# A four-layer kernel: layer 2's mixing reordered with its slot inputs one quarter ahead, its row sums moved a step earlier, and layer 3's value products paired

## The chip, the cores and the metric

The kernel runs on one core of a Trainium2 chip, as one program. The metric is the device time in microseconds (us). The profile is one execution of that program, recorded by the hardware profiler; "the span" is the time from its first to its last recorded instruction. The engines are named as the profile names them: PE (matmul) with PEld (its weight loads), DVE (vector), ACT (scalar), POOL (GpSimd) and SP (which here issues DMAs). Each engine executes its own queue in order; a semaphore makes one wait for another.

## What is computed

2,048 tokens of 512 channels go through four layers, each of the form x = x + ffn(cond(x)): attention with experts (layer 0), 32 experts with 4 chosen per token (layer 1), a soft mixture of experts (layer 2), and attention over a paged cache with an int8 product (layer 3). The change lies in the end of layer 1 and in layers 2 and 3; their lines are these, cut:

```python
# layer 1, the last step: every token sums its K = 4 expert rows
outs = outs[inv].reshape(-1, K, Hh)
y = jnp.sum(outs * topk_weight[..., None], axis=1)
# layer 2, cond: a base product and a low-rank adapter per sequence
H = jnp.einsum('btd,od->bto', x, W);  xa = jnp.einsum('btd,brd->btr', x, A_b)
delta = jnp.einsum('btr,bor->bto', xa, B_b) * s_b
# layer 2, ffn: 16 experts of 128 slots
logits = jnp.einsum('bnd,des->bnes', x_n, mu_n)
dispatch = jax.nn.softmax(logits, axis=1)                      # over a sequence's tokens
combine = jax.nn.softmax(logits.reshape(B, N, E * S), axis=-1) # over all slots
slot_in = jnp.einsum('bnd,bnes->besd', x_ln, dispatch)
h = gelu(jnp.einsum('besd,edh->besh', slot_in, W1) + b1)
slot_out = jnp.einsum('besh,ehd->besd', h, W2) + b2
out = jnp.einsum('bsd,bns->bnd', slot_out, combine)
# layer 3: scores over the gathered cache, softmax, values
o = jnp.einsum('bghts,bgsd->bghtd', softmax(scores), v_all)
```

In the kernel a tile holds two sequences of 64 tokens; layer 2 runs over 16 tiles and, within a tile, over its 16 experts in four quarters of four.

## The kernel before

**Tiles and layers.** The stream is 16 tiles of 128 tokens by 512 channels, kept in DRAM between layers. Layers 0 and 1 run first. Layer 1 leaves the experts' rows in DRAM (`ys`), and layer 2 sums them when it fetches a tile: tile load `xt` on SP, four gathers `yk` of 128 rows on POOL, and four adds on DVE, x += gate * yk (L1295 in `fetch` and `add`; L1280 in `combined`, which does the first two tiles at the head of layer 2 before anything else). The gathers' buffers `yk` are four, the tiles' buffers `xt` three.

**Layer 2** (`layer2`, L1752) is a loop of 17 steps. Step i works on two tiles at once: the first half of tile i (its softmaxes) and the second half of tile i - 1 (its mixing), while the base product and norm of tile i + 1 (`Lora`, `l2_norm_pieces`) run between. Most instructions are pinned, so that each engine's queue stands nearly as the source has it. The rest is placed by a scheduler. A step is, on PE:

- **logits**: four quarters of 16 matmuls `lp` (L1995), each scaled, maximised and exponentiated behind it (DVE L2000 to L2021, ACT L2024); two transposes `ep` (L2081) of the other tile's softmax come between.
- **hidden**: four quarters `zp` of 4 matmuls (L2072) for the other tile; DVE reads each into `z` (L2074). The bank `zp` has two buffers. Between them stand `tp2` (L2039), the highest logit of each row, from which DVE makes `dg` (L2043), and `bp` (L2049), the product with `dg` that spreads it. In this part, too, stand the four adds of the tile that is being fetched: two behind `z` 0, two behind `dg`.
- **mixing** of the other tile: `csum` and `dp` (the softmax's total), and for each quarter q: `turn(q)` (`ep`, copied to `ew` by ACT, L2083), `dispatch(q)` (`hp`, 8 matmuls, L2104, then two GELUs into `h` on ACT, L2109), `combine(q)` (`gp`, 16 matmuls, L2127, copied to `gT` by DVE, L2131) and `project(q)` (4 matmuls `out` of 128x512, L2138). `hp` and `gp` have one buffer each, `ew` and `gT` two, `h` three (each quarter uses two). Between them stand `Lora` and the pieces of the next norm: DVE L1957 to L1965, POOL L396 and L1967 (times gamma, plus beta), ACT L1972 (the square), POOL L396, DVE L1975 to L1978.

The order of the mixing is written out by hand (L1817 to L1889), in short: combine 0, dispatch 1, turn 3, project 0, combine 1, dispatch 2, project 1, combine 2, dispatch 3, project 2, combine 3, the transpose of the next tile, the bias product (L2143), project 3.

In its free stretches POOL also copies cache rows for layer 3 (`cache_rows`, `kvst`: a gather, then a store by SP; one buffer).

**Layer 3** (`Attend`, L2587) is a software pipeline of 64 steps, one for each sequence and pair of head groups. Step s does on PE: `kp`, the transposed keys of step s + 3; `pT`, the transposed probabilities of step s (`turn0`, `turn1`; six buffers `pTs`); `sp`, the scores of step s + 2; one output product `y` (L2700); and `op`, the value product of step s - 1 (L2678: three chunks for each of two heads, into one bank), which ACT copies to `oT` (L2681).

**Branches.** After layers 0 and 1 a conditional block (L1061) handles the pairs beyond the experts' capacity; here there are none, and all engines branch over it. Three tiles before the end of the expert stage `hint` (L315) marks the branch as likely taken on PE, DVE, ACT and POOL.

Of the kernel before, what the change touches and what calls it, by code (L numbers as in the profile page):

```python
# [10 lines left out]
F32 = mybir.dt.float32  # L11
# [5 lines left out]
ALU = mybir.AluOpType  # L17
# [4 lines left out]
P = 128  # L22
B, T, D = 32, 64, 512
NT = B * T // P
# [6 lines left out]
E1, K1, V1 = 32, 4, 56  # L31
# [218 lines left out]
class Prog:  # L250
# [43 lines left out]
    def results(self, pool):  # L294
# [16 lines left out]
                )  # L311

        return step

    def hint(self, label):  # L315

        traced = self.nc.cur_bb.bb.instructions
        before = len(traced)
        kinds = mybir.EngineType
        self.tc.mark_branch_hint_location(  # L320
            label, "LikelyTaken", (kinds.PE, kinds.DVE, kinds.Activation, kinds.Pool)
        )
        for ins in list(traced)[before:]:
            self.pin(SimpleNamespace(ins=ins))

    def pin(self, ins):

# [528 lines left out]
class Moe:  # L856
# [193 lines left out]
    def beyond(self):  # L1050
# [7 lines left out]
            number[0:1, 0:1], min_val=0, max_val=N * K,  # L1058
            skip_runtime_bounds_check_because="the number of pairs is at most N * K",
        )  # L1060
        with tc.If(n > 0, label=f"beyond{E}"), ExitStack() as ctx:  # L1061
            sb = ctx.enter_context(tc.tile_pool(name=f"vs{E}", bufs=1))
            ps = ctx.enter_context(tc.tile_pool(name=f"vps{E}", bufs=2, space=PSUM))
            iota = g.c("iota")
# [90 lines left out]
    def run(self, xs, per_tile):  # L1155
# [7 lines left out]
        with ExitStack() as ctx:  # L1163
# [77 lines left out]
            for u in range(len(self.units)):  # L1241
                k = 0
# [51 lines left out]
        def add(x, yk, gate):  # L1294
            g.pin(nc.vector.scalar_tensor_tensor(x, yk, gate, x, ALU.mult, ALU.add))  # L1295

        combined.fetch, combined.moe = fetch, self
        return combined
# [453 lines left out]
def layer2(g, w, combined, first, w3):  # L1752
    tc, nc, a = g.tc, g.nc, g.a
    with ExitStack() as ctx:
# [8 lines left out]
        x = [combined(sb, 0, 3), combined(sb, 1, 3)]  # L1763
# [20 lines left out]
        for i in range(NT + 1):  # L1784
            soft = Softmaxes(g, w, sb, s2, ps, xnT) if i < NT else None
            mix = Mix(g, w, sb, s2, ps, x[i - 1], *last) if last else None
            adds = []
            if len(x) < NT and i != 1:
                t, adds = combined.fetch(sb, max(i + 1, 2), 3)
                x.append(t)  # L1790
            if mix and not soft:
                mix.turn(0)
# [18 lines left out]
            if early:  # L1811
                lora.turn()
                mix.sums()
                lora.adapter()
                soft.highest()
                soft.divide(3)
                mix.dispatch(0)  # L1817
                norm = l2_norm_pieces(g, w, sb, s2, lora.product())
                next(norm)
                mix.total()  # L1820
                soft.over_slots()
                mix.turn(2)
                mix.combine(0)
                mix.dispatch(1)
            else:
                if z:
                    z.hidden(0)
                if soft:
                    soft.divide(3)
                for add in adds[0:2]:  # L1830
                    add()
# [5 lines left out]
                for add in adds[2:4]:  # L1837
                    add()
                if z:
                    z.hidden(2)  # L1840
                if soft:
                    soft.over_slots()
                if z:
                    z.hidden(3)
                    next(rows, None)
            if mix and not early:
                if lora:
                    lora.turn()
                mix.sums()
                mix.dispatch(0)  # L1850
                if lora:
                    lora.adapter()
                mix.turn(2)
                if lora:
                    norm = l2_norm_pieces(g, w, sb, s2, lora.product())
                    next(norm)
                    if i + 2 == NT:

                        w3["w_kv3"] = first.tile([P, 4, D], F32, name="w_kv3", tag="sb_w_2")
                        g.dma(w3["w_kv3"], a["w_kv3"])  # L1860
                        w3["x3"] = [first.tile([P, D], F32, name="x3", tag=f"sb_{k}") for k in ("w_a", "w_b")]
                        for j in range(2):
                            g.dma(w3["x3"][j], xs[j * P : (j + 1) * P, :])
                mix.total()
                mix.combine(0)
                mix.dispatch(1)
            if mix:
                mix.turn(3)
                if lora:
                    next(norm)  # L1870
                mix.project(0)
                next(rows, None)
                mix.combine(1)
                if lora:
# [7 lines left out]
                mix.combine(3)  # L1882
            before = xnT, nn
# [171 lines left out]
class Mix:  # L2055
# [76 lines left out]

    def project(self, q):
        g, nc, w = self.g, self.g.nc, self.w
        if q == 0:
            self.out = self.ps.tile([P, D], F32, name="out2", tag="acc", bufs=1)
        for e in range(4):
            g.first(e, nc.tensor.matmul(  # L2138
                self.out, self.gTs[q][:, e, :], w["w2"][:, 4 * q + e, :], start=q + e == 0, stop=q + e == 6 and q == 3
            ))  # L2140

    def bias(self):
        self.g.pin(self.g.nc.tensor.matmul(self.out, self.cs, self.w["b2"], start=False, stop=False))  # L2143

    def finish(self, xs, xb, i):
        g, nc, x = self.g, self.g.nc, self.x
# [208 lines left out]
def layer3(g, w, xs, xb):  # L2355
# [3 lines left out]
    with ExitStack() as ctx:  # L2359
# [159 lines left out]
        for s in range(-3, last + 8):  # L2519
# [67 lines left out]
class Attend:  # L2587
# [79 lines left out]
    def values(self, s):  # L2667

        nc = self.g.nc
        i, gp, half = self.where(s)  # L2670
        if s % 4 == 0:
            self.oT[i] = self.sb.tile([P, 2, 2, P], F32, name="oT", bufs=3)
        kv, pT = self.kvs[2 * i + half], self.pT.pop(s)
        op = self.ps.tile([P, P], F32, name="op", tag="op", bufs=1)
        for c in range(3):
            for j in range(2):
                at = 256 + (2 * gp + j) * 64
                nc.tensor.matmul(  # L2678
                    op[64 * j : 64 * j + 64, :], kv[c][:, at : at + 64], pT[j][:, c, :], start=c == 0, stop=c == 2
                )  # L2680
        nc.scalar.copy(  # L2681
            self.oT[i][:, gp, :, 64 * half : 64 * half + 64], op.rearrange("p (h t) -> p h t", h=2)
        )
        if half:
            self.products += [partial(self.product, i, 2 * gp + k) for k in range(2)]

    def out(self):

# [76 lines left out]
```

## Time and profile before

| what | us |
|---|---|
| median of 3 runs (lowest to highest) | 2591.81 (2587.51 to 2593.32) |
| the profiled execution: its time | 2598.3 |
| the profiled execution: its span | 2596.5 |
| head of layer 2, 1140.0 to 1228.0: PE busy | 67.6 of 88.0 |
| layer 2, the steps of tiles 1 to 14, 1292.6 to 2113.8: PE busy | 800.8 of 821.2 |
| layer 3, the attention steps, 2329.3 to 2596.5: PE busy | 253.9 of 267.2 |
| the same stretch: DVE busy, ACT busy | 209.9, 163.1 |

The page has six parts: busy time by engine, the span in 40 slices, DMA queues, the chain of work that ended last, the costliest groups of instructions, and DMA issues. A row of the timeline has the start in us, the time from the first to the last of the instructions merged in it, the engine, the line, the operation, out<-in, their number, and in brackets how long the engine was idle before it and what released it. Every matmul of this kernel appears as two passes, so 4 matmuls are x8 in a row. A PE row's length runs to the modelled end of its last pass, which lies a little behind the start of the next row; where PE time is counted here, it is from the start of one row to the start of the next.

### The profile page before, as it was taken

To read this page: it belongs to the slowest core of one execution; us is meant where nothing else is said; L and a number is where in the kernel's file an instruction comes from. 1 tells how busy PE (TensorE), PEld (TensorE's weight loads), DVE (VectorE), ACT (ScalarE), POOL (GpSimd) and SP (SyncE) were. 2 spreads that over 40 slices of the span, in tenths; PEclk is the share of its full clock that TensorE was granted. 3 is DMA by queue.
4 is the path that set the end of the run, shared out by engine and by line. 5 is a ranking of instruction groups with operands and counts; after the bars stand their busy time and mean duration, and the time that the engine had idled before them with its cause. 6 is when DMAs were issued, how large, how long until landed. Compare 5 with 4: busy or idle time off the path is not lost.

```text
span 2596.5 us, 42488 instructions
## 1 busy us (share of the span) xinstructions
PE 2447.1 (94%) x16582; PEld 1617.0 (62%) x16597; DVE 1411.3 (54%) x3470; ACT 718.1 (28%) x1512; POOL 904.0 (35%) x961
## 2 busy tenths in 40 slices
PE   6999979998799999979999999999999999979998
PEld 4777766666566666747666666666666665445554
DVE  4666646833745554447444444444444442657886
ACT  2444521112211111102222222222222221246664
POOL 2223225504144444523333333333333312563440
PEclk9999989998889999989999999999999999989999
DMA  2335225535456976844222222222222314424441
GB/s 102 108 120 186 92 98 181 190 103 194 162 198 227 362 273 238 283 128 148 72 72 72 72 75 68 79 72 72 75 73 74 96 56 138 167 58 132 134 136 46
DMA packets 132568, 339.39 MB, mean 131 GB/s; under 512 B 23993, under 2 KB 25049, under 8 KB 125056
## 3 DMA queue, kind: packets, MB, share of 16 engines
q1 hardware_dynamic: 90720, 188.84, 21.2%
q0 software_dynamic: 41056, 141.89, 17.2%
q10 hardware_dynamic: 576, 5.77, 0.6%
q8 instruction: 136, 2.23, 0.3%
q14 instruction: 80, 0.66, 0.1%
HBM read 245.23 MB, written 107.22 MB: 136 GB/s over the span
## 4 chain that ended last, share of the span: by engine, by line
PE 43%; DVE 10%; issue 2%; POOL 1%; DMA 0%; ACT 0%; another core or an unknown queue 0%; POOLq 0%; ACTq 0%; SPq 0%; DVEq 0%
PE out L2138 9%; PE lp L1995 7%; PE gp L2127 3%; PE pp L2452 3%; PE zp L2072 3%; PE yp L1938 2%; PE y L2700 2%; PE hp L2104 2%; PE op L2678 2%; PE sp L2631 2%; PE pT L2653 2%; DVE xt L1295 1%; PE ep L2081 1%; DVE inv L2031 1%; PE kp L2604 1%
## 5 line engine op out<-in xcount | busy, mean ns | idle before, releaser
L1202 PE MATMUL gu<-xT,wt 128*128 128x320 f32 (+5 forms) x1536 | 397.7, 406 | 4.6 <-DVE xT L1189 3.6
L1202 PEld LDWEIGHTS gu<-xT,wt 128*128 128x128 f32 x1536 | 283.6, 193 | 118.9 <-issue 49.1
L2138 PE MATMUL out<-sb_w,gT 128*128 128x512 f32 x512 | 233.6, 599 | 11.0 <-DVE nn L1975 6.5
L1995 PEld LDWEIGHTS lp<-xnT,sb_mu 128*128 128x128 f32 x2048 | 233.4, 192 | 9.3 <-issue 6.7
L1995 PE MATMUL lp<-xnT,sb_mu 128*128 128x128 f32 x2048 | 236.4, 275 | 2.1 <-DVE xnT L344 1.4
L2072 PE MATMUL zp<-sb_w,xnT 128*128 128x512 f32 x512 | 228.5, 595 | 3.6 <-DVE z L2074 3.6
L1217 PE MATMUL y<-wt,hT 128*128 128x512 f32 (+2 forms) x544 | 201.6, 599 | 2.7 <-DVE yo L1225 2.1
L372 POOL DMA_INDIRECT kvst<-kv,gidx x96 | 96.5, 1005 | 278.9 <-DMA oldkv<-kvst 194.0
L2131 DVE COPY gT<-gp 128x512 f32<-128x512 f32 x64 | 44.2, 691 | 246.0 <-PE gp L2127 245.6
L2138 PEld LDWEIGHTS out<-sb_w,gT 128*128 128x128 f32 x512 | 93.2, 190 | 116.1 <-issue 95.2
L2072 PEld LDWEIGHTS zp<-sb_w,xnT 128*128 128x128 f32 x512 | 93.7, 190 | 111.6 <-issue 99.5
L372 POOL DMA_INDIRECT kvt<-newkv,oidx x96 | 100.4, 1046 | 132.4 <-DMA kvt<-oldkv 77.8
L372 POOL DMA_INDIRECT yk<-ys,slot x96 | 97.5, 1015 | 116.3 <-DVE pre L1307 74.5
L2109 ACT ACTIVATE h<-hp 128x512 f32<-128x512 f32 x128 | 69.5, 595 | 213.6 <-PE hp L2104 213.5
L1217 PEld LDWEIGHTS y<-wt,hT 128*128 128x128 f32 (+2 forms) x544 | 73.3, 167 | 65.6 <-issue 52.4
L372 POOL DMA_INDIRECT xr<-rows,stok x101 | 98.2, 972 | 40.4 <-issue 18.3
L852 POOL TENSOR_TENSOR ga<-ga,sg 128x288 f32<-128x288 f32 (+5 forms) x66 | 50.8, 770 | 173.6 <-ACT sg L848 171.6
L2149 POOL TENSOR_TENSOR xt<-xt,bc_bias 128x512 f32<-128x512 f32 x16 | 20.2, 1264 | 220.5 <-DMA x<-xt 208.4
L2000 DVE TENSOR_TENSOR lT<-lp,cmu 128x512 f32<-128x512 f32 x64 | 43.5, 680 | 93.8 <-PE lp L1995 92.8
L2033 POOL TENSOR_TENSOR eT<-eT,inv 128x512 f32<-128x512 f32 x64 | 71.8, 1123 | 54.3 <-DVE inv L2032 46.2
L2127 PEld LDWEIGHTS gp<-lT,h 128*64 128x64 f32 x2048 | 65.0, 138 | 38.9 <-issue 25.9
L2024 ACT ACTIVATE eT<-eT 128x512 f32<-128x512 f32 x64 | 40.3, 630 | 173.9 <-DVE eT L2021 154.2
(458 smaller groups left out, 4642.9 us busy)
## 6 DMA issues: line engine op xcount, KB each, us to landing
ys<-yo SPq DMA_DIRECT2D x106, 256.0 KB
oldkv<-kvst SPq DMA_DIRECT2D x96, 224.0 KB
kvt<-oldkv SPq DMA_DIRECT2D x96, 224.0 KB
ys<-zero SPq DMA_DIRECT2D x10, 2048.0 KB
xt<-x SPq DMA_DIRECT2D x62, 256.0 KB
x<-xt SPq DMA_DIRECT2D x48, 256.0 KB
wt<-w_e SPq DMA_DIRECT2D x7, 1536.0 KB
sb_w<-w SPq DMA_DIRECT2D x5, 1024.0 KB
```

The costliest lines, as they stand in the source:

```text
L372: ins = self.nc.gpsimd.indirect_dma_start(out=out, out_offset=None, in_=src, in_offset=bass.IndirectOffsetOnAxis(ap=idx, axis=0), **kw)
L1202: follow(nc.tensor.matmul(o, wj[:, c, ic * P : (ic + 1) * P], xTs[u][:, c, 0:n], start=c == 0, stop=c == 3))
L1217: follow(nc.tensor.matmul(y[row : row + n, :], hTs[e][:, ic, col : col + n], wd[:, ic, :], start=ic == 0, stop=ic == 1,))
L1938: g.first(c, nc.tensor.matmul(yp, self.xT[:, c, :], w["w_2"][:, c, :], start=c == 0, stop=False))
L1995: g.first(e + c, nc.tensor.matmul(lp[:, e, :], w["mu"][:, c, (4 * q + e) * P : (4 * q + e + 1) * P], self.xnT[:, c, :], start=c == 0, stop ...
L2033: g.pin(nc.gpsimd.tensor_tensor(e3, e3, inv.unsqueeze(2).to_broadcast([P, 8, T]), ALU.mult))
L2072: g.first(c, nc.tensor.matmul(zp, self.xnT[:, c, :], w["w1"][:, c, cols], start=c == 0, stop=c == 3))
L2104: g.first(e + b, nc.tensor.matmul(hp[:, b, e, :], self.ews[q][r, e, :], self.z[q][r, e * P : (e + 1) * P], start=True, stop=True))
L2109: g.pin(nc.scalar.activation(self.hs[q][b], hp[:, b], AF.Gelu))
L2127: g.first(e + b + k, nc.tensor.matmul(gp[r, e, cols], self.hs[q][b][:, e, r], self.lT[q][:, e, cols], start=True, stop=True))
L2138: g.first(e, nc.tensor.matmul(self.out, self.gTs[q][:, e, :], w["w2"][:, 4 * q + e, :], start=q + e == 0, stop=q + e == 6 and q == 3))
L2452: nc.tensor.matmul(pp, xT[i][:, c, :], (w["w_kv3"] if z else wq)[:, c, :], start=c == 0, stop=c == 3)
```

## The change

- **Mixing.** The order becomes: dispatch 1, combine 0, the bias product, turn 3, dispatch 2, combine 1, project 0, dispatch 3, combine 2, project 1, combine 3, project 2, the transpose, project 3. The bias product now opens the accumulation (start=True) and project 0 no longer does. The early branch (step 1) and the other steps share it.
- **Row sums.** Step i fetches tile i + 2 (before: tile i + 1, and none at step 1). In steps from 1 on the adds stand in the mixing: behind the norm's first piece, behind combine 1, ahead of dispatch 3 and behind combine 3; at step 0 they stay in the hidden part. Three gathers go out at the fetch; the fourth is issued behind the first add. `yk` has three buffers instead of four (in `combined` too), `xt` four instead of three.
- **Layer 3.** `values` runs at even steps only, for two steps at once: 12 matmuls into one bank of twice the width, one ACT copy of 256 columns instead of two of 128.
- **Branches.** `hint` and the branch's label are gone.

As built, the orders of PE and DVE in a step are those of the source. On ACT, where the square of the norm (L1972) is not pinned, the order in the mixing changes from "GELUs of 1, `ew` 3, square, GELUs of 2" to "GELUs of 1, square, `ew` 3, GELUs of 2". On POOL the fourth gather stands behind the norm's last operation and ahead of two `kvst` gathers, and the other three open the step. On SP the load of tile 3 moves up next to that of tile 2, and every later one by one step.

```diff
-        with tc.If(n > 0, label=f"beyond{E}"), ExitStack() as ctx:
+        with tc.If(n > 0), ExitStack() as ctx:
...
-                if t == self.tiles - 3:
-                    g.hint(f"beyond{E}")
...
-                yk = pool.tile([P, D], F32, name="yk", bufs=4 if K == K1 else 6)
+                yk = pool.tile([P, D], F32, name="yk", bufs=3 if K == K1 else 6)
...
             adds = []
-            for k in range(K):
-                yk = pool.tile([P, D], F32, name="yk", bufs=4)
+
+            def rows(k):
+                yk = pool.tile([P, D], F32, name="yk", bufs=3)
                 g.gather(yk, self.ys, self.slot[:, i, k : k + 1], later=True)
-                adds.append(partial(add, x, yk, self.gates[:, i, k : k + 1]))
+                adds.append(partial(add, yk, k))
+
+            def add(yk, k):
+                g.pin(nc.vector.scalar_tensor_tensor(x, yk, self.gates[:, i, k : k + 1], x, ALU.mult, ALU.add))
+                if len(adds) < K:
+                    rows(len(adds))
+
+            for k in range(3):
+                rows(k)
             return x, adds
...
-            if len(x) < NT and i != 1:
-                t, adds = combined.fetch(sb, max(i + 1, 2), 3)
+            if len(x) < NT:
+                t, adds = combined.fetch(sb, i + 2, 4)
...
-                mix.combine(0)
-                mix.dispatch(1)
...
                 mix.total()
+            if mix:
+                mix.dispatch(1)
                 mix.combine(0)
-                mix.dispatch(1)
-            if mix:
-                mix.turn(3)
                 if lora:
                     next(norm)
-                mix.project(0)
+                add(0)
+                mix.bias()
+                mix.turn(3)
+                mix.dispatch(2)
                 next(rows, None)
                 mix.combine(1)
+                add(1)
+                mix.project(0)
+                add(2)
+                mix.dispatch(3)
+                mix.combine(2)
                 if lora:
                     xn = next(norm)
-                mix.dispatch(2)
                 mix.project(1)
-                mix.combine(2)
-                mix.dispatch(3)
-                mix.project(2)
                 next(rows, None)
                 mix.combine(3)
+                add(3)
+                mix.project(2)
...
             if mix:
-                mix.bias()
                 mix.project(3)
...
-            if 0 <= s - 1 <= last:
-                f.values(s - 1)
+            if s % 2 == 0 and 0 <= s - 2 <= last:
+                f.values(s - 2)
```

More of the change, by code (lines that the diff above doesn't have):

```diff
@@ L313, in results @@
         return step
[L315 to L324, printed above, removed]
     def pin(self, ins):
@@ L1287, in fetch @@
             adds = []
-            for k in range(K):
-                yk = pool.tile([P, D], F32, name="yk", bufs=4)
+            def rows(k):
+                yk = pool.tile([P, D], F32, name="yk", bufs=3)
                 g.gather(yk, self.ys, self.slot[:, i, k : k + 1], later=True)
-                adds.append(partial(add, x, yk, self.gates[:, i, k : k + 1]))
+                adds.append(partial(add, yk, k))
[5 more added lines that the diff above has]
+                rows(k)
             return x, adds
-        def add(x, yk, gate):
-            g.pin(nc.vector.scalar_tensor_tensor(x, yk, gate, x, ALU.mult, ALU.add))
         combined.fetch, combined.moe = fetch, self
@@ L1762, in layer2 @@
         xs, xb = g.stream("x2"), g.stream("x2b")
-        x = [combined(sb, 0, 3), combined(sb, 1, 3)]
+        x = [combined(sb, 0, 4), combined(sb, 1, 4)]
         for k in ("gamma", "beta"):
@@ L1787, in layer2, with add @@
             adds = []
-            if len(x) < NT and i != 1:
-                t, adds = combined.fetch(sb, max(i + 1, 2), 3)
+            def add(k):
+                if k < len(adds):
+                    adds[k]()
+            if len(x) < NT:
+                t, adds = combined.fetch(sb, i + 2, 4)
                 x.append(t)
@@ L1829, in layer2 @@
                     soft.divide(3)
-                for add in adds[0:2]:
-                    add()
+                if i == 0:
+                    add(0)
+                    add(1)
                 if z:
@@ L1836, in layer2 @@
                     soft.highest()
-                for add in adds[2:4]:
-                    add()
+                if i == 0:
+                    add(2)
+                    add(3)
                 if z:
@@ L1864, in layer2 @@
                 mix.total()
+            if mix:
+                mix.dispatch(1)
                 mix.combine(0)
-                mix.dispatch(1)
-            if mix:
-                mix.turn(3)
                 if lora:
                     next(norm)
-                mix.project(0)
+                add(0)
+                mix.bias()
+                mix.turn(3)
+                mix.dispatch(2)
                 next(rows, None)
                 mix.combine(1)
+                add(1)
+                mix.project(0)
+                add(2)
+                mix.dispatch(3)
+                mix.combine(2)
                 if lora:
                     xn = next(norm)
-                mix.dispatch(2)
                 mix.project(1)
-                mix.combine(2)
-                mix.dispatch(3)
-                mix.project(2)
                 next(rows, None)
                 mix.combine(3)
+                add(3)
+                mix.project(2)
             before = xnT, nn
@@ L2134, in project @@
         g, nc, w = self.g, self.g.nc, self.w
-        if q == 0:
-            self.out = self.ps.tile([P, D], F32, name="out2", tag="acc", bufs=1)
         for e in range(4):
             g.first(e, nc.tensor.matmul(
-                self.out, self.gTs[q][:, e, :], w["w2"][:, 4 * q + e, :], start=q + e == 0, stop=q + e == 6 and q == 3
+                self.out, self.gTs[q][:, e, :], w["w2"][:, 4 * q + e, :], start=False, stop=q + e == 6 and q == 3
             ))
     def bias(self):
-        self.g.pin(self.g.nc.tensor.matmul(self.out, self.cs, self.w["b2"], start=False, stop=False))
+        self.out = self.ps.tile([P, D], F32, name="out2", tag="acc", bufs=1)
+        self.g.pin(self.g.nc.tensor.matmul(self.out, self.cs, self.w["b2"], start=True, stop=False))
     def finish(self, xs, xb, i):
@@ L2669, in values @@
         nc = self.g.nc
-        i, gp, half = self.where(s)
-        if s % 4 == 0:
+        i, gp, _ = self.where(s)
+        if gp == 0:
             self.oT[i] = self.sb.tile([P, 2, 2, P], F32, name="oT", bufs=3)
[L2673 to L2680, printed above, removed]
+        op = self.ps.tile([P, 2, P], F32, name="op", tag="op", bufs=1)
+        for half in range(2):
+            kv, pT = self.kvs[2 * i + half], self.pT.pop(s + half)
+            for c in range(3):
+                for j in range(2):
+                    at = 256 + (2 * gp + j) * 64
+                    nc.tensor.matmul(
+                        op[64 * j : 64 * j + 64, half, :], kv[c][:, at : at + 64], pT[j][:, c, :],
+                        start=c == 0, stop=c == 2,
+                    )
         nc.scalar.copy(
-            self.oT[i][:, gp, :, 64 * half : 64 * half + 64], op.rearrange("p (h t) -> p h t", h=2)
+            self.oT[i][:, gp].rearrange("p h (b t) -> p b h t", b=2), op.rearrange("p b (h t) -> p b h t", h=2)
         )
-        if half:
-            self.products += [partial(self.product, i, 2 * gp + k) for k in range(2)]
+        self.products += [partial(self.product, i, 2 * gp + k) for k in range(2)]
     def out(self):
```

## Prediction

> **What bounds the kernel now.** I read the page first, then the busy time by stretches, then PE's waits in layer 2, then the timeline of one step of layer 2 engine by engine.
>
> ```profile
> PE 2447.1 (94%) x16582; PEld 1617.0 (62%) x16597; DVE 1411.3 (54%) x3470; ACT 718.1 (28%) x1512; POOL 904.0 (35%) x961
> ...
> PE   6999979998799999979999999999999999979998
> ...
> PEclk9999989998889999989999999999999999989999
> ```
>
> PE is the bound, at nearly full clock: an edit counts by the PE gaps it closes or opens. The stretches show where they are.
>
> ```profile
> 1292.60:2113.80 821.20, 800.82 (x6025) 531.56 (x6024) 397.91 (x704) 197.83 (x327) 257.37 (x256) 1.00 0.24 74
> ```
>
> The first number is the length, the second PE's busy time: 20.4 us of gap in 13 steps of layer 2. PE's waits in layer 2 (total, times, longest) name them:
>
> ```profile
> PE bp L2049 <- DVE dg L2043: 6.6, 13, 0.5
> PE out L2138 <- DVE nn L1975: 6.5, 12, 0.6
> PE out L2138 <- DVE gT L2131: 4.5, 9, 0.6
> PE zp L2072 <- DVE z L2074: 3.6, 11, 0.5
> ```
>
> The two `out` rows are one wait: the copy `gT` stands just ahead of `nn`. PE's timeline of one step (tile 7's hidden part and mixing) gives the price of each, start to start:
>
> ```profile
> 1658.48 3.70 PE L2072 MATMUL zp<-sb_w,xnT 128*128 128x512 f32 x8 [0.27 <-DVE z L2074]
> 1662.69 0.46 PE L2049 MATMUL bp<-dg,sb_cst 128*128 128x128 f32 x2 [0.50 <-DVE dg L2043]
> 1662.98 3.60 PE L2072 MATMUL zp<-sb_w,xnT 128*128 128x512 f32 x8
> 1666.42 0.60 PE L1917 MATMUL tp<-sb_cst,xt 128*128 128x128 f32 x4
> ...
> 1676.07 1.16 PE L2104 MATMUL hp<-z,ew 64*128 64x128 f32 x16
> 1677.16 0.66 PE L2081 MATMUL ep<-sb_cst,eT 128*128 128x128 f32 x4
> ...
> 1682.26 1.16 PE L2104 MATMUL hp<-z,ew 64*128 64x128 f32 x16
> 1683.95 3.70 PE L2138 MATMUL out<-sb_w,gT 128*128 128x512 f32 x8 [0.53 <-DVE nn L1975]
> ```
>
> A `zp` quarter takes 3.44 when nothing waits (1662.98 to 1666.42) and 4.21 ahead of `bp`: 0.77 lost. A dispatch `hp` takes 1.09 (1676.07 to 1677.16) and 1.69 when project follows it and waits for `gT`: 0.60 lost.
>
> **Part by part.** Sums are against the profiled execution (2598.3: span 2596.5 and 1.8 around it, 6.5 above the median). Its row lengths are taken for all steps; the difference then goes onto the median.
>
> *Mixing order.* Before, project q stands one dispatch (1.09) behind combine q, too little for the copy's latency (1.15 from `gp`'s start to its last read) plus 0.69 for the copy. After, project 0 has dispatch 2 and combine 1 ahead of it, project 1 dispatch 3 and combine 2 (and so on), over 3.5 us behind its own combine. All 21 waits go: 21 x 0.60 = -12.6. No matmul is added. A full-width `out` quarter takes 3.63 when a combine follows (1690.31 to 1693.94) and 3.43 when `lp` follows; such turns to small tiles fall from three to two a step, since project 2 is now followed by the transpose. 16 x 0.19 = -3.0. The new pair dispatch-then-combine has no row; its reverse costs nothing (`gp` 1.08 for 32 passes in either case), and I take nothing. The nearest worse row, `csum` ahead of `hp`, 1.01 where 32 passes of 0.027 are 0.87, would make it +0.14 x 3 x 16 = +7; it is a bound.
>
> *Row sums.* Without the adds, DVE's queue behind `z` 0 is: one sum, `z` 1, `mr`, `dg`. `z` 1's matmuls end near 1658.2, so `dg` ends near 1660.5 and `bp` can start at 1658.48 + 3.44 = 1661.92. The wait goes: 13 x 0.77 = -10.0. The `zp` wait for `z` 0 (3.6 by its row) stays: it comes from `eT` L2021 ahead of it, not from the adds. The adds' data are not late: gathers now lie some 35 us ahead of them. POOL's fourth gather starts about 8.5 us into the mixing and is used at about 17. The `kvst` gathers behind it move by about 1 us, and they wait for their own store anyway (5.3 us each). The tile load moves up one step on SP; with four buffers it waits for the same earlier tile's store as before, and what is queued behind it (cache stores) has the same wait ahead of it. All nothing.
>
> *What is late next.* In the mixing ACT now stands at the norm's square, and `ew` 3 and the GELUs of 2 are queued behind it; dispatch 3 on PE waits for both (`hp` has one bank). These are the chain's present rows:
>
> ```profile
> 1677.67 1.27 POOL L1967 TENSOR_TENSOR xl<-xl,bc_gamma 128x512 f32<-128x512 f32 x1 [0.95 <-DVE xl L1965]
> 1679.02 1.26 POOL L1967 TENSOR_TENSOR xl<-xl,bc_beta 128x512 f32<-128x512 f32 x1
> ```
>
> ```profile
> 1680.31 0.63 ACT L1972 ACTIVATE sq<-xl 128x512 f32<-128x512 f32 x1 [1.47 <-POOL xl L1967]
> 1680.85 0.19 ACT L1972 ACTIVATION_READ_ACCUMULATOR sq<-xl 128x1 f32 x1
> ```
>
> From the start of `dp` (1674.78) PE comes to dispatch 3 at 0.21 + 1.09 + 1.08 (combine 0) + 0.86 (bias) + 0.49 + 1.09 + 1.08 + 3.53 = 9.43. DVE makes `gT` 0 ahead of `xl`; combine 0 now starts at 1.30, so `gT` 0 at 2.49, `xl` 3.10 to 3.90, gamma at 3.98, beta at 5.33, the square at 6.62 to 7.35, `ew` 3 to 7.94, the GELUs to about 9.0. Margin 0.4. But the first add now starts as `xl` ends, beside gamma, and the second may meet beta. Where an add started 0.26 ahead of POOL's `eT` (1659.17, 1659.43), POOL took 1.39 instead of 1.04: +0.35. [...] I take 0.15 x 14 = +2.1; bounds 0 and 0.6 x 14 = +8.4. The other new waits fit: the second GELU of 1 needs combine 0's end (three `h` buffers), about 2.5, and is done near 3.1, where dispatch 2 starts at 3.73.
>
> *Three `yk` buffers at the head.* In the timeline gathers start at 1146.04, 1147.33, 1148.57, 1149.82; the fifth waits for the first add and starts at 1151.50. Each is added about 3.75 behind its start. With three buffers the fourth starts at 1151.50: +1.7 to tile 0 and to PE, which waits for it (15.9 before `tp` L1917). At step 0 the fourth gather stands behind POOL's `eT`s, which end at 1196.44, so its row lands near 1200.2 and the last add starts 1.3 later than 1198.91; `z` 2, the four subtractions and the `xnT` copy stand behind it on DVE, and `lp` already waits 1.45 for that copy: +1.3.
>
> *Hints.* With the hint, PE's branches at 596 and 1140 resolve in 0.4 and it is past them at once, while DVE, ACT and POOL still stand 4.2, 3.9 and 3.6 behind the branch at 1140. [...] At 1140 PE has nothing to do until 1154.47, and the others already pay: nothing. At 596 PE, ACT and POOL could lose up to 4.2; DVE already stands until 599.2, and PE's next work starts at 599.52, so a PE held from 595.9 by 4.2 is 0.6 late. I take +0.7, bounds 0 and +8.4 (4.2 at both).
>
> *Layer 3.* The same matmuls, regrouped. ACT loses 64 copies of 0.265 and gains 32 of about 0.37 (by the slope to `kT`, 336 columns in 0.44): 5 us of an engine at 163 of 267, so nothing. `pTs` has six buffers, and six are live at an even step's end: enough. A cache buffer of an even sequence comes free one step (4 us) later; its gather stands four steps behind its load. The PE steps become alternately 0.81 shorter and longer; DVE needs about 3.3 a step (209.9 over 64) against a shortest step of 2.9, and catches up in the long one. I take 0, bounds -4 (half of PE's listed waits there, 7.7 us) and +6 (0.2 at each short step).
>
> **Sum:** -12.6 - 3.0 - 10.0 + 2.1 + 1.7 + 1.3 + 0.7 = -19.8; 2591.8 - 19.8 = 2572.0.
>
> **Rivals.** *Half the gain* (chance 0.25): the waits for `gT` only change their name: dispatch 3 stands for the GELUs behind the square at the upper bound, +8.4 instead of +2.1, and the small-tile pairs cost half their bound, +3.5: 2572.0 + 9.8 = 2582. For it: ACT's order as built, and a margin of 0.4. *Layer 3 and the branches at their bounds* (0.10): +6 and +7.7 more: 2586. For it: DVE's load there; against it: the wait list of PE in that stretch names DVE for only 5 us. *Slower* (0.14): the norm's chain is late as a whole. Everything behind the square on ACT then holds PE, 1 us per us, in 14 steps. POOL would be the cause: the root L396 stands in its queue behind a `kvst` gather that waits for a store. Beyond 9.43 + (19.8 + 2.1)/14, that is with the GELUs ending 11.0 behind `dp`, the gain is gone; at 11.5 the kernel takes 2599. Against it: the last such gather ends at 1668.4, the root starts at 1676.2, so 7.7 us are spare. That the change does less than it says (the `dg` wait remaining by another queue) is within the second case.
>
> **Numbers.** The likeliest, 2572 (chance 0.51), has 2565 to 2579 of its own. The range 2565 to 2592 takes in the half gain and the third case and leaves out most of the slower case and a little below. Faster by over 0.2% means below 2586.6, and 0.2% is about what a measurement of this kernel can tell: 0.75; within it, 0.12; slower 0.13.
>
> **What would show it.** The PE rows `bp <- dg` and `out <- gT` or `nn` vanish from the waits, `hp` is 1.09 everywhere, step length falls from about 63.7 to 62.3. If dispatch 3 stalls, a row `hp <- ACT h` or `ew` appears in 14 places. `tp` L1917 starts at about 1156 instead of 1154.5. If PE's busy time, not its gaps, grows in the mixing, the small-tile pairs cost. Wrong altogether would be steps that keep 63.7.

## The result and the profile after

After: 2564.3 us median of 4 runs (2562.9 to 2568.9). Before, beside it: 2592.4 of 4 (2587.5 to 2593.3). The ratio is 0.9898, 95% interval 0.9880 to 0.9916. By the medians the kernel is 28 us faster where 19.8 were predicted, 0.7 below the low end of the range; the ratio, taken on the prediction's 2591.8, gives 2565.4, just inside it. The profiled execution of after took 2568.9 (span 2567.1), 29.4 less than the one of before.

Lines after the change lie two further down in layer 2 (`hp` L2106, `gT` L2133, `bp` L2051, `zp` L2074); `out` stays L2138, `op` is L2680, `y` L2702. The page of after:

```profile
PE 2430.8 (95%) x16597; PEld 1624.3 (63%) x16597; DVE 1408.3 (55%) x3470; ACT 715.5 (28%) x1480; POOL 908.4 (35%) x961
```

PE is busy for 16 us less, though it issues the same matmuls. The stretches show where (length first, then the busy time of PE, PEld, DVE, ACT and POOL, the granted PE clock, the DMA share and GB/s). Layer 3 from the first value product to the last, then the twelve steps of layer 2 from the second `dp` to the fourteenth, of before:

```profile
2329.30:2583.40 254.10, 248.73 (x1802) 143.79 (x1817) 204.87 (x705) 162.25 (x480) 87.65 (x81) 1.00 0.37 112
1292.60:2056.80 764.20, 744.90 (x5583) 493.69 (x5581) 370.91 (x654) 185.62 (x306) 241.50 (x240) 1.00 0.24 73
```

and of after:

```profile
2309.60:2554.00 244.40, 239.02 (x1803) 147.08 (x1804) 204.00 (x696) 153.64 (x441) 88.04 (x81) 0.99 0.41 117
1295.40:2034.20 738.80, 738.80 (x5582) 495.96 (x5581) 365.22 (x654) 188.38 (x306) 243.10 (x237) 1.00 0.24 74
```

Layer 2's steps are 25.4 shorter, and PE has no gap left in them: every step takes 61.57, where nearly all of before's took 62.8 to 64.1. Layer 3 is 9.7 shorter, and there it is PE's busy time that fell (248.73 to 239.02); its gaps are the same 5.4. The rest of the run adds 5.6: layers 0 and 1, whose code only lost the hints and one buffer, -4.7 (two profiles of before differ by 8.9 there), the head of layer 2 +7.1, smaller pieces +3.2. PE's waits in layer 2 of after (total, times, longest):

```profile
PE hp L2106 <- ACT h L2111: 3.9, 3, 1.8
PE lp L1997 <- DVE xnT L333: 2.9, 1, 2.9
PE bp L2051 <- DVE dg L2045: 1.3, 1, 1.3
PE pp L2453 <- ACT xT L331: 1.0, 2, 0.8
PE ep L2083 <- DVE rd L2118: 0.9, 1, 0.9
```

None of the four rows that the prediction showed is left but one `bp`, of step 0. The `zp` row is gone too, which the prediction had staying. The `hp` row has three places, not fourteen: steps 1, 15 and 16. One step's rows, start to start, with ACT's GELUs:

```profile
1587.76 3.60 PE L2074 MATMUL zp<-sb_w,xnT 128*128 128x512 f32 x8
1591.20 0.38 PE L2051 MATMUL bp<-dg,sb_cst 128*128 128x128 f32 x2
...
1611.38 1.09 ACT L2111 ACTIVATE h<-hp 128x512 f32<-128x512 f32 x2
1612.89 1.16 PE L2106 MATMUL hp<-z,ew 64*128 64x128 f32 x16
```

`zp` takes 3.44 ahead of `bp` (4.21 before). Dispatch 3 (1612.89) starts 0.42 after the GELUs end (1612.47): it doesn't stall.

### The profile page after: what moved, and what is told of

It reads as the page before. It is cut to its first block, busy times and chain, and to the rows that moved or that the text cites. A ratio compares the mean times of both kernels' runs of the same rounds, so it can differ in the third digit from the quotient of the medians.

```text
span 2567.1 us, 42539 instructions
## 1 busy us (share of the span) xinstructions
PE 2430.8 (95%) x16597; PEld 1624.3 (63%) x16597; DVE 1408.3 (55%) x3470; ACT 715.5 (28%) x1480; POOL 908.4 (35%) x961
## 4 chain that ended last, share of the span: by engine, by line
PE 50%; DVE 2%; POOL 1%; issue 1%; DMA 1%; ACT 0%; SPq 0%; ACTq 0%; POOLq 0%; DVEq 0%
PE out L2138 9%; PE lp L1997 8%; PE zp L2074 8%; PE pp L2453 3%; PE hp L2106 3%; PE gp L2129 3%; PE y L2702 2%; PE yp L1940 2%; PE sp L2632 2%; PE pT L2654 2%; PE op L2680 2%; PE ep L2083 1%; PE kp L2605 1%; PE ap L1928 1%; PE out L2144 1%
## 5 line engine op out<-in xcount | busy, mean ns | idle before, releaser
L2138 PE MATMUL out<-sb_w,gT 128*128 128x512 f32 x512 | 234.9, 602 | 0.0
L2074 PE MATMUL zp<-sb_w,xnT 128*128 128x512 f32 x512 | 226.5, 592 | 0.0
L2074 PEld LDWEIGHTS zp<-sb_w,xnT 128*128 128x128 f32 x512 | 93.7, 190 | 104.8 <-issue 102.2
L2138 PEld LDWEIGHTS out<-sb_w,gT 128*128 128x128 f32 x512 | 92.2, 190 | 96.1 <-issue 92.8
L2133 DVE COPY gT<-gp 128x512 f32<-128x512 f32 x64 | 44.2, 691 | 168.2 <-PE gp L2129 168.2
L2085 ACT COPY ew<-ep 128x512 f32<-128x512 f32 x64 | 37.2, 583 | 200.5 <-PE ep L2083 193.9
L2643 ACT ACTIVATE s<-s,m 128x336 f32<-128x336 f32 x128 | 72.7, 569 | 46.0 <-DVE m L2639 39.7
```

Of the source, the lines that this page charges most:

```text
L2074: g.first(c, nc.tensor.matmul(zp, self.xnT[:, c, :], w["w1"][:, c, cols], start=c == 0, stop=c == 3))
L2138: g.first(e, nc.tensor.matmul(self.out, self.gTs[q][:, e, :], w["w2"][:, 4 * q + e, :], start=False, stop=q + e == 6 and q == 3))
L2643: nc.scalar.activation(p, p, AF.Exp, bias=m, scale=-1.0, accum_out=tot)
```

## The experiments

The runs fall into two groups. In the one, called A here, before takes 2592 to 2596 us; the result above belongs to it. In the other, B, the same program takes 2549. Each kernel is compared with the runs of before in its own group, and some kernels ran in both. What a group stands for isn't known. The expectations below call it a chip, but the chip numbers on record are 1 and 4 for B and 1 and 7 for A (the result above has none): 1 stands on both sides. The granted clock doesn't set them apart; it was 0.97 to 0.98 in both.

### Each part alone, on B

*mix_only*: before, with the order of the mixing and the bias product of after.

```diff
+                mix.dispatch(1)
                 mix.combine(0)
-                mix.dispatch(1)
...
+                mix.bias()
                 mix.turn(3)
-                mix.project(0)
+                mix.dispatch(2)
                 mix.combine(1)
+                mix.project(0)
```

> The kernel before with the new order of the mixing alone (bias product first); fetch, adds, hints and layer 3 as before. By the prediction's terms: -12.6 for the 21 waits for gT and -3.0 for two small-tile turns instead of three, so -15.6; dispatch 3 has no add beside the norm's chain and does not stall. By the trace of the changed kernel, in which a mixing gained about 10 of the 12.6 + 3.0 because the fewer turns gave nearly nothing: about -12.5. Rival, if the mixing and the sums share a cause (the whole quarter ahead needs DVE free of the adds): under -8. PE's waits for bp (6.6) and zp (3.6) should stay as before in all of these.

Measured: 2553.8 against 2549.0, ratio 1.0024 (1.0014 to 1.0034): slower, by 5 us. PE's waits in layer 2:

```profile
PE hp L2102 <- ACT h L2107: 3.9, 3, 1.8
...
PE bp L2047 <- DVE dg L2041: 0.7, 3, 0.3
```

The `hp` row of after comes with the order. The `bp` row should have been 6.6. It is 0.7, in a kernel that has the adds where before has them.

*sums_only*: before, with the row sums moved.

```diff
-            if len(x) < NT and i != 1:
-                t, adds = combined.fetch(sb, max(i + 1, 2), 3)
+            if len(x) < NT:
+                t, adds = combined.fetch(sb, i + 2, 4)
...
                     next(norm)
+                add(0)
                 mix.project(0)
```

> The kernel before with only the row sums moved: fetch of tile i + 2, four tile buffers and three row buffers, the adds in the old mixing at the places that answer to the new ones. By the prediction: the bp wait goes, -10.0, the zp wait for z 0 stays, head and step 0 cost +3.0, so -7.0. By the rival that the adds also hold z 0 (through the eT that meets POOL's, or through DVE's whole queue): -15.5 + 3.0 = -12.5, and the row zp <- DVE z is gone from the waits. If the adds now delay the gT copies of the old, tight order, some of it comes back as longer out <- gT waits: up to 13 x 0.66 = +8.6.

Measured: 2549.4, ratio 1.0005 (0.9995 to 1.0014): the same. Neither reading fits.

*pairs_only*: before, with layer 3's paired values.

```diff
-            if 0 <= s - 1 <= last:
-                f.values(s - 1)
+            if s % 2 == 0 and 0 <= s - 2 <= last:
+                f.values(s - 2)
```

> The kernel before with only layer 3's value products paired. By the prediction 0 (bounds -4 and +6). By the rival read from the changed kernel's trace, where the stretch from the first value product to the last took 244.4 instead of 254.1: -9 to -10, with PE's busy time in it lower by about 5 (24 passes in 1.46 instead of 2 x 0.81 = 1.62, 32 times) and its gaps lower by about 4.

Measured: 2539.8, ratio 0.9965 (0.9952 to 0.9977): -9. The rival was right in the sum, not in its split: from the first value product to the last PE is busy for 235.43 of 238.2, where mix_only, with layer 3 as before, has 248.82 of 250.7. So all that fell is PE's busy time; the gaps did not. And the layer 2 of pairs_only, which is that of before, took 740.4 for the twelve steps, where before had shown 764.2. So the layer 2 waits of the prediction do not come with the program alone.

*adds_back*: after, with the adds of every step in the hidden part.

```diff
-                if i == 0:
-                    add(0)
-                    add(1)
+                add(0)
+                add(1)
...
-                add(1)
                 mix.project(0)
-                add(2)
```

> The changed kernel with the adds of every step back in the hidden part (two behind z 0, two behind dg), still fetched one step earlier; all else as changed. By the prediction the bp wait returns and only it: +10.0. By the rival (the adds hold z 0 as well): +15.5, with the rows bp <- dg near 6.6 and zp <- z near 3.6 both back. If neither comes back, it was the new order or the earlier gathers that removed them, and the time stays within 2 us of the changed kernel's.

Measured: 2556.8, ratio 1.0032 (1.0019 to 1.0045) against before; after itself has 0.9982 on B (below), so this is some 13 us slower than after. The expected rows didn't come back, others came. DVE's own waits, in steps 1 to 13:

```profile
DVE xt L1282 <- DMA yk<-ys,slot: 18.3, 11, 3.4
```

and PE's:

```profile
PE ap L1922 <- ACT fT L1915: 8.0, 12, 1.3
```

With three buffers the fourth gather is issued behind the first add, and in the hidden part its row is needed before it has landed. So this run says nothing on `z` 0. It does show that the three buffers need the adds in the mixing.

### The two kernels once more

> The kernel before, unchanged, for its trace on the chip of the experiments (2549 there, 2592 where the prediction was made). If the 21 gT waits, the 13 bp waits and the 11 zp waits belong to the kernel, they are there again: layer 2 from the second dp to the fourteenth in about 764 us, steps of 63.7. If they hang on the moment at which POOL's kvst gathers fall against the gT copies and POOL's eT against DVE's lT, as the trace of the kernel with layer 3 alone changed suggests (its untouched layer 2 ran those steps in about 61.7), they are gone here too: about 740 us, no out <- gT row.

This run fell on A, a single one: 2593.0. Waits `bp` 6.6, 13 times; `out` 6.5 and 4.6; `zp` 2.7; the twelve steps 763.3. So the waits come again on A; on B a program with the same layer 2 (pairs_only) hasn't them.

> The changed kernel, unchanged, on the chip of the experiments. If the prediction's gains belong to the kernel: 28 us below before, near 2521. If the layer 2 waits are absent from before on this chip: layer 3's -9 stays, layer 2 gives at most the rest of the bp wait (about 0.3 x 13 = -4), the head and step 1 cost +3 to +6, so between -10 and -4 against before.

Measured: 2565.6 against 2595.6, ratio 0.9884 (0.9867 to 0.9900): the result repeats on A.

*hints_back*: after, with the branch hints of before.

```diff
-        with tc.If(n > 0), ExitStack() as ctx:
+        with tc.If(n > 0, label=f"beyond{E}"), ExitStack() as ctx:
```

> The changed kernel with the branch hints back. By the prediction -0.7 against the changed kernel (a branch on PE of 0.4 instead of 3.6 to 4.0 us, but only 0.6 of it uncovered at the branch after layer 0). [...]

Measured: 2565.8, ratio 0.9883 against after's 0.9884. The hints are worth nothing that can be told here. In the traces PE's next row behind the branch of layer 0 starts 3.9 (after_again) and 4.3 (after) behind it without the hint and 3.6 with it.

### What holds the copy

The trace of pairs_only beside that of before answers it. Before, on A, at the second quarter of one mixing:

```profile
1681.18 1.15 PE L2127 MATMUL gp<-lT,h 128*64 128x64 f32 x32
...
1681.87 0.99 POOL L372 DMA_INDIRECT kvst<-kv,gidx  x1 [0.21 <-issue]
...
1683.21 0.69 DVE L2131 COPY gT<-gp 128x512 f32<-128x512 f32 x1 [5.62 <-PE gp L2127]
...
1693.94 1.15 PE L2127 MATMUL gp<-lT,h 128*64 128x64 f32 x32
...
1695.14 0.69 DVE L2131 COPY gT<-gp 128x512 f32<-128x512 f32 x1 [4.88 <-PE gp L2127]
```

The copy of quarter 3 starts 1.20 behind its combine, the copy of quarter 1 2.03 behind. DVE had been idle for 5 us in both. What differs is the `kvst` gather on POOL, 0.51 ahead of the point where the copy could start (1682.38). The same place in pairs_only, on B:

```profile
1653.47 1.15 PE L2127 MATMUL gp<-lT,h 128*64 128x64 f32 x32
...
1654.17 0.99 POOL L372 DMA_INDIRECT kvst<-kv,gidx  x1 [0.20 <-issue]
1654.67 0.69 DVE L2131 COPY gT<-gp 128x512 f32<-128x512 f32 x1 [4.79 <-PE gp L2127]
```

The same 0.70 from combine to gather, and the copy starts on time. I counted this over layer 2: `gT` copies whose combine had ended between 0.2 and 1.3 behind the start of a `kvst` gather. On A, in four runs with the old order, 72 of 74 are late, and all but three of these start 1.3 to 1.4 behind the gather's start. On B, in four runs with the old order, none of 36. The small copy `csb` (L2096) does the same: 72 of 72 late in seven runs on A, none of 62 in seven on B.

*gT_scalar*: before, with another DVE operation for the copy.

```diff
-        g.pin(nc.vector.tensor_copy(self.gTs[q], gp))
+        g.pin(nc.vector.tensor_scalar(self.gTs[q], gp, 1.0, None, ALU.mult))
```

> The kernel before with one line changed: DVE makes gT by a multiplication with 1.0 (TENSOR_SCALAR) instead of a plain COPY. Nothing else moves. By the theory that a plain COPY on DVE cannot start from about 0.2 us behind the start of a gather on POOL until 0.35 behind its end, while other DVE operations can: the 21 delays of 0.83 go, -12.6 on the chip where before takes 2593, 0 on the one where it takes 2549. By the rival that it is the latency from combine to project as such (the prediction's reading), or any DVE instruction that writes SBUF: no change, the rows out <- gT stay at 11.

It fell on B: ratio 1.0007 (0.9995 to 1.0019), as both readings had it there. Then the same on A:

> The kernel before with gT made by TENSOR_SCALAR instead of COPY, once more, for a chip on which before takes about 2593. There, by the theory that only a plain COPY on DVE is held by a gather on POOL: the 21 delays of 0.83 go and with them the rows out <- gT, -12.6. By the rival (any DVE write at that place, or the latency as such): no change. On a chip where before takes 2549: 1.0007 again.

Measured on A: 2592.7 against 2593.3, ratio 1.0007 (0.9993 to 1.0021). My theory of a plain copy falls. The waits are all there:

```profile
PE bp L2049 <- DVE dg L2043: 6.6, 13, 0.5
PE out L2138 <- DVE nn L1975: 6.2, 12, 0.5
PE out L2138 <- DVE gT L2131: 3.9, 8, 0.6
```

and of its copies that met a gather, 22 of 23 are late in the same manner. It is not the operation; what is left is the gather.

### The row sums alone, on A

> The same as sums_only, for the chip on which before takes about 2593, if it lands there. There, by the prediction: -10.0 for bp, z 0 stays, +3.0 at the head: -7.0, with the out <- gT rows (11) still in PE's waits. By the rival that the move also shifts POOL (three gathers instead of four ahead of its first eT, which then no longer meets DVE's third lT): the zp rows go as well, -15.5 + 3.0 = -12.5; lT starts within 0.3 of POOL's eT instead of 1.1 behind it. On a chip where before takes about 2549 the same as before (1.0005) again.

It fell on B: 1.0012 (1.0005 to 1.0020). Then, on A:

> The row sums alone, once more, for a chip on which before takes about 2593. By the prediction -7.0 (bp gone, zp <- z stays, head +3.0), out <- gT stays at 11. By the rival that POOL's first eT no longer meets DVE's third lT: zp <- z goes too, -12.5. If the moved gathers also change where the kvst gathers fall against the gT copies, the out <- gT rows shrink as well, and it gains up to 25. On a chip where before takes 2549: 1.001 again.

Measured on A: 2569.7 against 2593.3, ratio 0.9910 (0.9883 to 0.9938). The row sums alone take 23 us (16 to 30 by the interval), where the prediction gave them 7. PE's waits in the steps:

```profile
PE gp L2144 <- ACT h L2126: 1.5, 2, 1.3
PE out L2155 <- DVE nn L1992: 0.5, 1, 0.5
PE out L2155 <- DVE gT L2148: 0.5, 1, 0.5
```

With the old order of the mixing, the waits for `gT` are gone, but for two. In its timeline (L2144 combine, L2148 copy, L2155 project):

```profile
1666.77 1.15 PE L2144 MATMUL gp<-lT,h 128*64 128x64 f32 x32
...
1667.87 1.02 POOL L372 DMA_INDIRECT yk<-ys,slot  x1 [0.18 <-issue]
1667.96 0.69 DVE L2148 COPY gT<-gp 128x512 f32<-128x512 f32 x1 [4.13 <-PE gp L2144]
1668.94 3.70 PE L2155 MATMUL out<-sb_w,gT 128*128 128x512 f32 x8
1669.20 0.93 POOL L372 DMA_INDIRECT kvst<-kv,gidx  x1 [0.31 <-issue]
```

The fourth `yk` gather, which now stands behind the norm, has pushed the `kvst` gather 1.3 us on. The copy starts 1.19 behind its combine, 0.09 behind the start of one gather and ahead of the next, and project follows at once. The two copies that are still late met a `kvst` gather 0.52 and 0.59 after its start.

The `zp` wait goes the same way. Before, on A, at the third `lT` of a step:

```profile
1646.76 0.93 POOL L372 DMA_INDIRECT kvst<-kv,gidx  x1 [0.30 <-issue]
1647.70 1.06 POOL L2033 TENSOR_TENSOR eT<-eT,inv 128x512 f32<-128x512 f32 x1
1648.87 0.69 DVE L2000 TENSOR_TENSOR lT<-lp,cmu 128x512 f32<-128x512 f32 x1 [1.61 <-PE lp L1995]
```

and the same place in pairs_only, on B:

```profile
1620.18 0.93 POOL L372 DMA_INDIRECT kvst<-kv,gidx  x1 [0.30 <-issue]
1621.11 0.69 DVE L2000 TENSOR_TENSOR lT<-lp,cmu 128x512 f32<-128x512 f32 x1 [0.43 <-PE lp L1995]
1621.13 1.06 POOL L2033 TENSOR_TENSOR eT<-eT,inv 128x512 f32<-128x512 f32 x1
```

On B `lT` starts 0.93 behind the gather's start, its matmuls being done. On A, in the three runs with the fetch of before, it starts 1.9 to 2.1 behind it in nearly every step, 1.0 to 1.2 late, and the softmax behind it, with `z` 0 and `dg`, is that much later. In sums_third three `yk` gathers instead of four stand ahead of that `kvst`:

```profile
1693.84 0.93 POOL L372 DMA_INDIRECT kvst<-kv,gidx  x1 [0.30 <-issue]
...
1695.77 1.04 POOL L2050 TENSOR_TENSOR eT<-eT,inv 128x512 f32<-128x512 f32 x1 [1.01 <-DVE inv L2049]
1696.03 0.69 DVE L2017 TENSOR_TENSOR lT<-lp,cmu 128x512 f32<-128x512 f32 x1 [0.44 <-PE lp L2012]
```

The gather is 1.25 earlier against `lT`, which starts 2.19 behind it and on time, and it does so 0.26 into an `eT` of POOL. So an `eT` of POOL alone, which my expectation had named, doesn't hold it; the gather is again what stands there. But this case is less clear than that of the copy. `lT` starts some 0.6 later behind the gather's start than `gT` does (1.3 to 1.4). In 11 of the twelve steps of before it starts within 0.11 of the end of the POOL `eT` that began just when `lT` could have (above: 1647.70 + 1.06 = 1648.76, and `lT` at 1648.87). Whether the gather alone does it, or the gather and then the `eT` behind it, stays open.

What wasn't run: the order of the mixing alone on A, adds_back on A, and a kernel that moves only the `kvst` gathers. So that the gather holds DVE on A is supported by where the late instructions lie, and by the delay's going when the gather moves with the row sums; it is not shown by moving the gather alone. A kernel with the row sums and the pairs and the old order wasn't run either. From the lengths of the steps in after against sums_third on A (+1.1 over the twelve steps, +1.7 in the first, +1.7 in the last, -1.0 in the one before it) it would be some 3.5 us faster than after, which is an estimate.

### After, on B

> The changed kernel, unchanged, for the chip on which before takes about 2549, if it lands there: layer 3's -9 stays, layer 2 gives nothing, the new mixing costs the +4.8 that it cost alone there: between -6 and -2 against before. If it beats before by 28 there too, the layer 2 gains do not hang on the chip. On the chip where before takes 2593: 0.989 once more.

Measured on B: 2544.0 against 2548.6, ratio 0.9982 (0.9975 to 0.9989). The change that takes 28 to 30 us on A takes 4.7 on B. The parts there are -9 (pairs), +5 to +6 (order), 0 to +3 (row sums); they sum to between -4 and 0, so the sum of the parts falls a little short of the whole.

## Why the prediction was right, and where it was wrong

The direction was right, and the total was short by 8 us. It came that near because errors of the split offset each other.

- **"Project q stands one dispatch (1.09) behind combine q, too little for the copy's latency" (the order, -12.6).** This step failed. A copy that nothing holds starts 1.20 behind its combine and takes 0.69: 1.89, where the old order gave 1.08 + 1.09 = 2.17. The order was enough; the other 0.83 of the copy's delay came where the gather stood. The trace of before had the counter-example: a mixing without a wait (from the `dp` at 1612.03), and the copy of quarter 3 in every step. With the row sums done, the order adds to the twelve steps rather than taking from them: 737.7 without it, 738.8 with it, both on A. Whether the order alone would have closed the waits on A, where it has slack enough for a late copy, stays open.
- **The three `out` turns (-3.0).** Wrong in sign. Without waits the old mixing takes 23.86 from `dp` to the end of `out` (pairs_only), the new one 23.97. The old order had one quarter at 3.53 and two at 3.63 already, and the new one has 3.63, 3.63 and 3.54. The bias product takes 0.96 ahead of a transpose where it took 0.86.
- **The row sums, -10.0.** The waits for `bp` went, as said. Together with what the move did to the gathers, which was not foreseen, the part alone measured -23 on A, its loss at the head included; the twelve steps are 26.5 shorter. How much of this is the adds and how much the softmax, which is no longer late, no run on A tells. That the adds alone hold `bp` is not so either: on B, with the adds where they were, the `bp` row is 0.7 in mix_only instead of 6.6.
- **The `zp` wait stays: "it comes from `eT` L2021 ahead of it, not from the adds".** Failed. That `eT` took 1.83 in the step shown in the prediction, and at the same place of pairs_only, on B, it took 1.64, where no `zp` row stands in the waits:

```profile
1655.14 1.83 DVE L2021 TENSOR_TENSOR eT<-lT,m 128x512 f32<-128x512 f32 x1
```

```profile
1627.63 1.64 DVE L2021 TENSOR_TENSOR eT<-lT,m 128x512 f32<-128x512 f32 x1
```

On A the softmax was late from its third `lT` on, beside a `kvst` gather, and the `yk` gathers ahead of that one belong to the part that moved. I had counted what the moved gathers wait for ("The `kvst` gathers behind it move by about 1 us", "All nothing"), and not what the `kvst` gathers do where they land.
- **Dispatch 3, +2.1.** Its bound of 0 held. The instants were near: the GELUs ended 9.26 behind `dp` (forecast about 9.0 without a meeting) and PE came at 9.68 (9.43). Gamma met the first add and took 1.71 instead of 1.27:

```profile
1607.04 0.74 DVE L1282 SCALAR_TENSOR_TENSOR xt<-yk,gates,xt 128x512 f32<-128x512 f32 x1
1607.20 1.71 POOL L1969 TENSOR_TENSOR xl<-xl,bc_gamma 128x512 f32<-128x512 f32 x1 [2.04 <-DVE xl L1967]
```

That is +0.44, where the row had said +0.35; 0.58 of the add was left when gamma began. No run shows the 0.15 a step that the sum takes, nor its bound of 0.6: a margin of 0.42 remained here, and dispatch 3 stalls in none of steps 2 to 14. The stalls came at steps 1, 15 and 16, which I hadn't worked out: 3.9 in all, where before had 1.6 of waits for `h` (under `gp`).
- **The head, +1.7 and +1.3.** Right in kind. On A it takes 17.1 to 17.9 from the branch to `tp` with the row sums moved, 14.5 to 15.1 without: +2.7, by the middles. The `lp` wait at step 0 is 2.9 for 1.45: +1.5.
- **The hints, +0.7.** PE's two branches last 4.0 and 3.6 in after (under PEld, `COMPARE_BRANCH`), where before's last 0.4, and PE's next row behind the first of them starts 0.3 to 0.7 later without the hint than with it. In the time 0 was measured (2565.6 without, 2565.8 with); the range of the measurement takes +0.7 in.
- **Layer 3, "The same matmuls, regrouped", 0.** The term was mis-sized: -10 on A, -9 on B. I looked for gaps and counted PE's work as unchanged. The rows show it change. Before, on A:

```profile
2451.47 1.02 PE L2700 MATMUL y<-sb_w_o,oT 128*128 128x512 f32 x2
2452.43 0.88 PE L2678 MATMUL op<-pTs,kvt 112*64 112x128 f32 x12
2453.24 0.51 PE L2604 MATMUL kp<-sb_cst,kvt 112*128 112x112 f32 x3
```

After, on A:

```profile
2487.38 1.02 PE L2702 MATMUL y<-sb_w_o,oT 128*128 128x512 f32 x2
2488.33 1.53 PE L2680 MATMUL op<-pTs,kvt 112*64 112x128 f32 x24
2489.80 0.51 PE L2605 MATMUL kp<-sb_cst,kvt 112*128 112x112 f32 x3
...
2500.82 0.45 PE L2605 MATMUL kp<-sb_cst,kvt 112*128 112x112 f32 x3
2501.11 0.49 PE L2654 MATMUL pT<-sb_cst,s 128*112 128x128 f32 x3
```

Start to start, 24 passes of `op` take 1.47 where twice 12 took 1.62, and `kp` behind `y` takes 0.29 where behind `op` it takes 0.34. A `y` takes about 0.95 ahead of `op` and 0.86 when `kp` follows (2499.96 to 2500.82). By these rows four steps lose 2 x (0.15 + 0.05 + 0.09) = 0.58 at the turns, and sixteen fours 9.3: an estimate, close to the 9.7 by which PE's busy time fell. This is the price that I had put on `out` (0.19 a turn to small tiles) and did not carry to layer 3.

So the total came near by luck in part: -15.6 for the order was too much by all of it, -10.0 for the row sums (-7.0 with their loss at the head) and 0 for the pairs too little by 16 and 10.

## What to carry to other kernels

When a wait names a late instruction, compare that instruction with its own kind where it is not late, and see what runs beside it, before the order of the work is blamed: here a third of the copies were late and two thirds were not. A gather that moved pushed the gather behind it in POOL's queue 1.3 us on, and which DVE operations the gathers met was part of the cost on A (a `gT` copy beside one was 0.83 late). And matmuls that were only regrouped still changed PE's time at the turns between shapes (24 passes of `op` took 1.47, twice 12 took 1.62): price each turn in every part of the kernel, by the same row. Last, one set of runs need not speak for another: the same change took 28 us in group A and 5 in group B.

## What was not expected of the hardware

The same program ran 1.7% apart in the two groups (2593 and 2549), at the same granted clock. Some 24 us of it lie in layer 2's steps (764, and 740 in pairs_only) and about 10 to 20 in layer 1, from the first branch to the second (534 to 544 and 521 to 526). In group A DVE's `gT` and `csb`, which start from idle, don't start until 1.3 to 1.5 us behind the start of a `kvst` gather, and in B they aren't late; their own durations (0.69 and 0.29) are the same. `lT` was late on A too, by 1.0 to 1.2. Nor does every gather hold every operation on A: the second `lT` of a step starts 0.69 behind a `yk` gather, and 0.04 behind the end of its matmuls: unheld. What sets the two groups apart, one chip from another or something else, stays open.
